# Ranks pinned to half-slots, x's first part loaded and normed first, and a second layer that sums messages with the columns on partitions

## The chip, the cores and the metric

The kernel runs on one core of a Trainium2 chip. The metric is the device time of one execution in microseconds (us). The core's engines are TensorE (PE in the profile; PEld is its weight loading), VectorE (DVE), ScalarE (ACT), GpSimd (POOL) and SyncE (SP, which only issues DMAs here). Each runs its own instructions in order; DMAs are issued from the queues of SP, ACT and POOL.

## The reference

x has 6250 nodes with 128 features. There are 106250 edges (50000 in both directions and a loop at each node), sorted by their destination, with 64 features and one of 4 types each. Everything is f32. Two layers follow each other, each behind a layer norm with ReLU and each added to x:

- The first is an attention over relations. For each of the 4 types, each of 8 heads has a logit for every edge from scores of its source and its destination; a softmax over the edges of one type into one node weighs the sources' rows, and the weighted rows are summed per node. A gelu, a product with W_cross and a second attention, over the node itself and the four types, make the node's output.
- The second makes a message of every edge and sums the messages of each node:

```
edge_in = concat([nf[src_full], nf[dst_full], ef_full])
msg = leaky_relu(edge_in @ We1) @ We2
red = segment_sum(msg, dst_full)
out = leaky_relu(concat([nf, red]) @ Wn1) @ Wn2
```

Here `src_full` is src followed by dst and `dst_full` is dst followed by src, so every edge sends a message both ways: one to its destination, by which the edges are sorted, and one to its source, by which they are not. The hidden layer of a message has 256 columns.

## The kernel before, in words

Nodes are cut into NU = 50 blocks (called units) of 126 nodes, each of two halves of 63 nodes on partitions 0 to 62 and 64 to 126. A half has up to 9 tiles (TB) of 128 edges, so there are 900 tiles. The first layer goes in NS = 25 steps of four halves. A scheduler orders the instructions of the engines from the program, within its pools of buffers; `keep_in_program_order` fixes an instruction's place among the others.

**Preparation.** SP loads src, dst, type and next destination (L161 to L239). x is loaded in 5 parts of 10 units, the first two on ACT's queue behind the weights, the rest on SP (L244 to L252). SP then writes tables to memory: e2 (L280, L281), turnd (where a node's edges end, six DMAs, L288 and L290), lacks (which edges are not of a type, four, L294) and dtyp (L297). From st0 (L345), the first edge of each half, SP reads registers (L165) and issues 100 loads of index tiles, ct (L356). The loop over the 50 units (L376 to L404) norms ten units at a time (`layernorm_relu`, L140 to L156, called at L382), transposes a unit (L384), copies it (L386), multiplies it with the weights of the four types and of the node itself (L391, L394), and writes the rows to xt on POOL's queue (L403) and the own row to memory on ACT's (L400). `columns` (L364 to L373) casts and transposes one ct tile in each of the last ten units and so makes xi, the indices that the first layer gathers with. DMAs of SP's and ACT's queues take turns on eight semaphores, so one may wait for the one before it on the same semaphore.

**First layer.** POOL issues one indirect gather of 128 rows of xt per tile (`gather0`, L85), 17 tiles ahead of their use (LA0). DVE, ACT and PE weigh them (`messages`, L603 to L618) and sum them per node. A tile of a step has two half-slots, (i, 0) inside `messages` and (i, 1) behind it, in which softmax pieces of the next step are put. Beside this the kernel works out where each message to a source shall be written in the second layer: `count` (L738), then 25 calls of `rank(g)` (L802), one for two units, each with three DVE instructions on 128x832 values, own_ (L805), a running sum (L807) and a predicated copy (L808); `ranked` (L810) ends it and writes the places (L823). `rank_at` (L825) gives the ranks to tiles (0 and, in odd steps, 5) of the steps from NCS on. Their place in the program does not keep the scheduler from moving them.

**Second layer.** For each unit and each of 9 positions there is a step with two tiles: POOL gathers rows of abtab, 7 positions ahead (AHEAD, L85), PE multiplies (L1105), DVE adds (L1107), ACT multiplies (L1108), DVE takes the maximum (L1109). The hidden row s has 512 columns, 256 for each direction. The 256 for the destination are summed at once, as a matmul with the one-hot oh (128 edges x 64 nodes) as the weights and s as the moving operand (L1125), both halves into one tile `sums` of 128 nodes x 256 columns. The 256 for the source are scattered by POOL to m2d (L1113), sorted by the places from the ranks. `windows` (L986) reads them back, part by part (DONE = 11, 22, 32, 43, 50), makes a one-hot ohw of 128 x 128 (L1015) and sums them with it as the weights (L1016). `add_sums` (L979) puts or adds a unit's sums to racc, 128 nodes x 256 columns per unit. `ready` (L1040) loads and prepares the next unit. Pieces of windows and ready are put between the steps by generators.

**Tail.** Behind the last scatter, the fifth part's windows run, and `node_update` (L905) runs for four units at a time: it transposes racc (8 transposes, L912, and 2 ACT copies to rT, L913), multiplies with We2 (L916), and makes the two layers of the node update (L922, L924, L930) and the output.

The two lines that sum messages:

```
nc.tensor.matmul(sums[q * 64:(q + 1) * 64, :], oh[:, q * TB + i, :], s[:, q, 0:HID],
                 start=(i == 0), stop=(i == TB - 1))                              # L1125
nc.tensor.matmul(sums, oh, mt[:, i, 0:HID], start=(i == 0), stop=(i == n - 1))    # L1016
```

The second operand is the weights, the third the moving operand; the output has the weights' columns on partitions.

Of the kernel before, what the change touches and what calls it, by code (L numbers as in the profile page):

```python
# [89 lines left out]
def kernel(ctx: ExitStack, tc: tile.TileContext, x, src, dst, ef, et, w_rel, a_src, a_dst,  # L90
# [107 lines left out]
    with ExitStack() as prep:  # L198
# [3 lines left out]


        wall = cpool.tile([P, R * XR + R * H + C + 2 * H], F32, name="wall")
        wx = wall[:, 0:R * XR].rearrange("p (r c) -> p r c", r=R)
# [34 lines left out]


        x_sb = cpool.tile([P, NU, C], F32, name="x_sb")
        for u0 in range(0, NU, 10):
            nc.gpsimd.memset(x_sb[:, u0:u0 + 10, :], 0.0)  # L244
            for q in range(2):
                n0 = u0 * DB + q * GB
                k = 10 if u0 + 10 < NU else 9
                xq = x[u0 * DB:(u0 + k) * DB, :].rearrange("(u q r) c -> q r u c", q=2, r=GB)[q]
                for r0, r1 in ((0, 48), (48, GB)):
                    (nc.scalar if u0 < 20 else nc.sync).dma_start(x_sb[q * 64 + r0:q * 64 + r1, u0:u0 + k, :], xq[r0:r1])  # L250
        for h, n in halves(NU - 1):
            nc.sync.dma_start(x_sb[h, NU - 1, :], x[n, :])  # L252

        nc.gpsimd.tensor_copy(wx[:, :, 0:C], wr)
# [28 lines left out]
        nc.vector.tensor_copy(dstf, ints["dst"])  # L283
        dn = cpool.tile([P, 2, J], BF16, name="dn")
        tt(dn[:, 1, :], ints["dst"], nxt, op=ALU.is_equal)
        ts_(dn[:, 0, :], dn[:, 1, :], -1.0, NEAR, op0=ALU.add, op1=ALU.mult)
        for k in range(2):
            nc.sync.dma_start(turnd[k, 1:JE + 1].rearrange("(p j) -> p j", j=J), dn[:, k, :])  # L288
            for o, w in ((0, 1), (JE + 1, 7)):
                nc.sync.dma_start(turnd[k:k + 1, o:o + w], dn[0:1, k, 0:w])  # L290
        for r in range(R):
            ne = wpool.tile([P, J], BF16, name="ne")
            ts_(ne, ints["et"], float(r), None, op0=ALU.not_equal)
            nc.sync.dma_start(lacks[r].rearrange("(p j) -> p j", j=J), ne)  # L294
        dty = cpool.tile([P, J], F32, name="dty")
        stt(dty, dstf, float(R), ints["et"], op0=ALU.mult, op1=ALU.add)
        nc.sync.dma_start(dtyp[0].rearrange("(p j) -> p j", j=J), dty)  # L297


# [59 lines left out]


        first = cpool.tile([P, NBK, TB], F32, name="first")
        nc.gpsimd.iota(first, [[GB, NBK], [0, TB]], base=0, channel_multiplier=0, allow_small_or_imprecise_dtypes=True)
# [13 lines left out]
        for u in range(NU):  # L376
            if u >= NU - NBK // CG:
                columns(u - NU + NBK // CG)
            if u % 10 == 0:
                h_sb = wpool.tile([P, 10, C], F32, name="h_sb")  # L380
                sq = wpool.tile([P, 10, C], F32, name="sq", bufs=1)
                layernorm_relu(wpool, h_sb, x_sb[:, u:u + 10, :], sq)  # L382
            tp = pp.tile([P, P], F32, name="tp")
            nc.tensor.transpose(tp, h_sb[:, u % 10, :], ident)  # L384
            hT = wpool.tile([P, P], F32, name="hT")
            nc.scalar.copy(hT, tp)  # L386
            row = wpool.tile([P, R * XR], F32, name="row", bufs=3)
            ps = pp.tile([P, 2, 512], F32, name="ps")
            xw = R * XR // 2
            for k in range(2):  # L390
                nc.tensor.matmul(ps[:, k, 0:xw], hT, wall[:, k * xw:(k + 1) * xw], start=True, stop=True)  # L391
            nc.vector.tensor_copy(row.rearrange("p (a c) -> p a c", a=2), ps[:, :, 0:xw])
            po = pp.tile([P, R * H + C + 2 * H], F32, name="po")
            nc.tensor.matmul(po, hT, wall[:, R * XR:], start=True, stop=True)  # L394
            for q in range(2):
                nc.scalar.copy(edbd[q * 64:(q + 1) * 64, u, q * 32:(q + 1) * 32], po[q * 64:(q + 1) * 64, 0:R * H])
            so = wpool.tile([P, SX], F32, name="so", bufs=3)
            nc.scalar.copy(so[:, 0:C + 2 * H], po[:, R * H:])
            nc.gpsimd.tensor_tensor(out=so[:, C + 2 * H:], in0=x_sb[:, u, :], in1=blb, op=ALU.add)
            nc.scalar.dma_start(own[u * P:(u + 1) * P, :], so)  # L400
            for q in range(2):
                n0 = u * DB + q * GB
                nc.gpsimd.dma_start(xt[n0 * R:(n0 + GB) * R, :].rearrange("(p r) c -> p (r c)", r=R),  # L403
                                    row[q * 64:q * 64 + GB, :])  # L404
# [36 lines left out]
    with ExitStack() as s1_:  # L441
# [360 lines left out]
        def rank(g):  # L802

            own_ = wp.tile([P, J], F32, name="own_", bufs=1)
            stt(own_, skey, float(g), sunit, op0=ALU.is_equal, op1=ALU.mult)  # L805
            place = wp.tile([P, J], F32, name="place", bufs=1)
            scan(place, own_, own_, base1[:, g:g + 1], op0=ALU.add, op1=ALU.max)  # L807
            nc.vector.copy_predicated(plc, own_.bitcast(I32), place)  # L808

# [14 lines left out]

        rank_at = [(s, i) for s in range(NCS, NS) for i in ((0, 5) if s % 2 else (0,))]  # L825

# [23 lines left out]
        for s in range(NS):  # L850
# [5 lines left out]
            if more:  # L856
                work(s + 1)
                for at, f in zip(((2, 0), (3, 1), (4, 0), (4, 1), (5, 0), (5, 1), (6, 0), (7, 0), (8, 0)), soft(s + 1)):
                    todo[at] = f
                for c in range(3):  # L860
                    todo[c, 1] = lambda c=c: logits(s + 1, c)
                gts.append(wp.tile([P, 2, R + 1], F32, name="gt", bufs=3))
            for i in range(TB):
                n = s * TB + i
                if n + LA0 < NS * TB:
                    gather0(n + LA0)
                messages(s, i, acc, turns_, todo.get((i, 0), lambda: None))
                todo.get((i, 1), lambda: None)()
                if more and i <= R:
                    tallies(s + 1, i, gts[s + 1])  # L870

                g = NC0 + s * TB + i
                if g < NU // 2:
                    count(g, True)
                if (s, i) == (NCS, 0):
                    counted()
                if (s, i) in rank_at[:NU // 2]:
                    rank(rank_at.index((s, i)))
                    if rank_at.index((s, i)) == NU // 2 - 1:
                        ranked()  # L880
                if i == 5 and s + 2 < NS:
                    loads(s + 2)
# [11 lines left out]
    c3 = fast.enter_context(tc.tile_pool(name="c3", bufs=1))  # L894
    racc = c3.tile([P, NU, HID], F32, name="racc")
    w2 = c3.tile([P, 2, C], F32, name="w2")
# [6 lines left out]
    def node_update(wp, pp, b0, nbs):  # L903
# [3 lines left out]
        nc.sync.dma_start(hT[:, 0:w], h2t[:, b0 * P:b0 * P + w])  # L907
        rT = wp.tile([P, 2, 4 * P], F32, name="rT")
        for a in range(2):
            tp = pp.tile([P, 4 * P], F32, name="tp")  # L910
            for i in range(nbs):
                nc.tensor.transpose(tp[:, i * P:(i + 1) * P], racc[:, b0 + i, a * P:(a + 1) * P], ident)  # L912
            nc.scalar.copy(rT[:, a, 0:w], tp[:, 0:w])  # L913
        ps = pp.tile([P, 4 * P], F32, name="tp")
        for a in range(2):
            nc.tensor.matmul(ps[:, 0:w], w2[:, a, :], rT[:, a, 0:w], start=(a == 0), stop=(a == 1))  # L916
        rdT = wp.tile([P, 4 * P], F32, name="rdT")
# [27 lines left out]
    with ExitStack() as s4:  # L945
# [33 lines left out]
        def add_sums(b, sums):  # L979

            if b in begun:
                tt(racc[:, b, :], racc[:, b, :], sums, op=ALU.add)
            else:
                nc.scalar.copy(racc[:, b, :], sums)
                begun.add(b)

        def windows(j):
# [17 lines left out]
            for b in range(NU):  # L1005
# [5 lines left out]
                ts_(at[:, 0:n], mt[:, 0:n, HID], float(-b * DB), None, op0=ALU.add)  # L1011
                sums = ps2.tile([P, HID], F32, name="sums2")
                for i in range(n):
                    oh = mp.tile([P, P], F32, name="ohw", bufs=4)
                    ts_(oh, col, at[:, i:i + 1], None, op0=ALU.is_equal)  # L1015
                    nc.tensor.matmul(sums, oh, mt[:, i, 0:HID], start=(i == 0), stop=(i == n - 1))  # L1016
                add_sums(b, sums)
                yield

        with ExitStack() as s5:  # L1020
# [64 lines left out]
            for u in range(NU):  # L1085
# [5 lines left out]
                if u in DONE[:-1]:  # L1091
# [5 lines left out]
                    taken = 0  # L1097
                sums = pt.tile([P, HID], F32, name="sums")
                for i in range(TB):
# [24 lines left out]
                    for q in range(2):  # L1124
                        nc.tensor.matmul(sums[q * 64:(q + 1) * 64, :], oh[:, q * TB + i, :], s[:, q, 0:HID],  # L1125
                                         start=(i == 0), stop=(i == TB - 1))
                    if u >= DONE[0]:
# [595 lines left out]
```

## Time and profile before

| what | us |
|---|---|
| median of 3 runs (lowest, highest) | 4111.01 (4106.76, 4119.22) |
| the profiled execution | 4104.87 |
| its span in the trace | 4103.1 |
| preparation, to the first gather | 0 to 158.7 |
| first layer, to its last gather | 158.7 to 1403.4 |
| between, to the second layer's first gather | 1403.4 to 1492.8 |
| second layer's steps, to the last scatter | 1492.8 to 3902.7 |
| tail | 3902.7 to 4103.1 |

Over the span PE is busy for 3053.0 us (74%), POOL for 2892.2 (70%), DVE for 2738.6 (67%), ACT for 1545.1 (38%). The bounds of the stages are the starts and ends of POOL's indirect DMAs in the trace. A group's line in the profile names the source line, the engine, the operation, its output and inputs and its shape, then the count, the busy time, the mean of one and the idle time of the engine just before it, with what ended that. In a timeline a line has the start, the length, and in brackets the idle time before it and what released it. Busy times of DMA instructions on POOL are the time in which POOL makes the descriptors; the names SPq and ACTq stand for the issue of a DMA.

### The profile page before, as it was taken

The numbers are of one execution on the slowest core, as the hardware profiler recorded it, in microseconds if no ns is written. First come the engines' busy times: TensorE is split into PE (matmuls) and PEld (weight loads), VectorE is DVE, ScalarE is ACT, GpSimd is POOL, SyncE is SP. The second block draws the span as 40 slices with busy tenths as digits, with TensorE's granted clock in tenths as the row PEclk, the third lists the DMA queues.
The fourth block names the chain that finished last, engine by engine and source line by source line (L and its number), as shares of the span: only waits on it lengthen the run. The fifth ranks groups of instructions, "written<-read, shape, count | busy, mean of one in ns | idle before, by whom it ended". The sixth has DMA issues, their size and how long they took to land. (4 is left out here: it accounts for less than half of the span.)

```text
span 4103.1 us, 43438 instructions
## 1 busy us (share of the span) xinstructions
PE 3053.0 (74%) x11258; PEld 1729.4 (42%) x11258; DVE 2738.6 (67%) x5139; ACT 1545.1 (38%) x2990; POOL 2892.2 (70%) x2887
## 2 busy tenths in 40 slices
PE   4468877778887756666678877778768777688888
PEld 3346555555555532222234342334324333244455
DVE  7467888887777745555466665666657666577755
ACT  3256655566666622222223333222222322222211
POOL 5777787777777527777777777777777777777600
PEclk9669978899999978888899898999989998899999
DMA  7544444455555356666587886888868878588754
GB/s 193 160 101 122 115 114 115 116 123 121 122 129 127 92 135 186 178 178 182 164 252 236 254 249 183 246 245 242 248 198 259 246 234 248 174 260 272 228 167 140
DMA packets 414557, 754.19 MB, mean 184 GB/s; under 512 B 182846, under 2 KB 249380, under 8 KB 414300
## 3 DMA queue, kind: packets, MB, share of 16 engines
q0 software_dynamic: 148800, 430.91, 35.8%
q1 hardware_dynamic: 234314, 290.32, 27.2%
q10 hardware_dynamic: 31186, 30.10, 2.6%
q8 instruction: 92, 1.51, 0.2%
q14 instruction: 165, 1.35, 0.1%
HBM read 586.37 MB, written 164.69 MB: 183 GB/s over the span
## 5 line engine op out<-in xcount | busy, mean ns | idle before, releaser
L85 POOL DMA_INDIRECT xg<-xt,xi x900 | 970.8, 1079 | 274.4 <-issue 224.6
L1113 POOL DMA_INDIRECT m2d<-s,placei x900 | 913.1, 1015 | 294.6 <-issue 211.4
L85 POOL DMA_INDIRECT ag<-abtab,srci x900 | 907.7, 1009 | 294.6 <-issue 205.4
L1105 PE MATMUL z<-rhs,lt 128*128 128x512 f32 x1800 | 1032.5, 701 | 0.6 <-ACT lt L1069 0.6
L1109 DVE TENSOR_TENSOR s<-s,z 128x1024 f32<-128x1024 f32 x450 | 548.1, 1220 | 549.1 <-ACT z L1108 547.7
L1125 PE MATMUL sums<-s,oh 128*64 128x256 f32 x1800 | 335.2, 455 | 491.3 <-DVE s L1109 490.6
L1107 DVE TENSOR_TENSOR s<-z,ag 128x1024 f32<-128x1024 f32 x450 | 549.8, 1222 | 198.8 <-PE z L1105 154.3
L617 PE MATMUL acc<-oh,msg 128*128 128x256 f32 x1800 | 534.3, 435 | 174.2 <-DVE oh L616 168.9
L1108 ACT ACTIVATE z<-s 128x1024 f32<-128x1024 f32 x450 | 461.1, 1025 | 414.8 <-DVE s L1107 413.5
L1105 PEld LDWEIGHTS z<-rhs,lt 128*128 128x128 f32 x1800 | 352.5, 216 | 447.9 <-issue 441.0
L1016 PE MATMUL sums<-mt,ohw 128*128 128x256 f32 x2024 | 523.3, 392 | 8.7 <-DVE ohw L1015 8.7
L1110 ACT COPY s<-srcf 128x2 f32<-128x2 f32 x450 | 86.7, 193 | 1175.8 <-DMA m2d<-s,placei 1159.9
L617 PEld LDWEIGHTS acc<-oh,msg 128*128 128x128 f32 x1800 | 365.2, 216 | 279.7 <-DVE oh L616 210.3
L1016 PEld LDWEIGHTS sums<-mt,ohw 128*128 128x128 f32 x2024 | 389.3, 198 | 198.0 <-issue 128.5
L1125 PEld LDWEIGHTS sums<-s,oh 128*64 128x64 f32 x1800 | 98.6, 149 | 727.6 <-DVE s L1109 579.4
L616 DVE TENSOR_SCALAR oh<-iota,key 128x256 f32<-128x256 f32 x900 | 307.6, 363 | 144.0 <-PE acc L617 136.0
L624 ACT ACTIVATE junk<-dt,nthr 128x1152 bf16<-128x1152 f32 x250 | 312.9, 1252 | 0.2
L1015 DVE TENSOR_SCALAR ohw<-col,at 128x128 f32<-128x128 f32 x1012 | 250.1, 302 | 15.6 <-PE sums L1016 7.9
L1069 ACT COPY lt<-tp 64x384 f32<-64x384 f32 x300 | 141.7, 472 | 108.0 <-PE tp L1065 55.8
L1065 PE MATMUL tp<-ident,fe 128*128 128x128 f32 x450 | 83.6, 292 | 125.5 <-ACT lt L1069 95.6
L607 DVE TENSOR_TENSOR msg<-xg,pw 128x512 f32<-128x512 f32 x225 | 150.8, 684 | 14.6 <-ACT pw L602 14.4
L542 ACT COPY es<-xg 128x128 f32<-128x128 f32 x225 | 62.1, 297 | 221.1 <-DMA xg<-xt,xi 175.8
(417 smaller groups left out, 3227.3 us busy)
## 6 DMA issues: line engine op xcount, KB each, us to landing
mt<-m2d SPq DMA_DIRECT2D x156, 514.0 KB
db<-in_dst_dram SPq DMA_DIRECT2D x200, 288.0 KB
mt<-m2d SPq DMA_DIRECT2D x53, 642.5 KB
dt<-dtyp SPq DMA_DIRECT2D x100, 288.0 KB
fe<-in_edge_attr_dram SPq DMA_DIRECT2D x100, 288.0 KB
mt<-m2d SPq DMA_DIRECT2D x41, 385.5 KB
xg<-xt,xi POOLq DMA_INDIRECT x900
ag<-abtab,srci POOLq DMA_INDIRECT x900
```

The lines of the kernel that those rows point to most:

```text
L85: nc.gpsimd.indirect_dma_start(out=o, out_offset=None, in_=table, in_offset=bass.IndirectOffsetOnAxis(ap=idx.bitcast(I32), axis=0))
L616: ts_(oh.rearrange("p t n -> p (t n)"), iota, key[:, k:k + 1], None, op0=ALU.is_equal)
L617: nc.tensor.matmul(acc[q // 2][:, :, q % 2, :], msg[:, q, :], oh, start=(i == 0 and q % 2 == 0), stop=(i == TB - 1), skip_group_check=True)
L624: nc.scalar.activation(junk, lanes[s]["dt"][v], AF.Sign, bias=nthr[:, u, t:t + 1], accum_out=g[:, v, t:t + 1])
L1015: ts_(oh, col, at[:, i:i + 1], None, op0=ALU.is_equal)
L1016: nc.tensor.matmul(sums, oh, mt[:, i, 0:HID], start=(i == 0), stop=(i == n - 1))
L1105: nc.tensor.matmul(z[:, q, :], lt[q][:, i * P:(i + 1) * P], rhs[(2 * u + q) % 4], start=True, stop=True)
L1107: tt(s[:, :, 0:2 * HID], z, ags.pop(n), op=ALU.add)
L1108: nc.scalar.mul(z, s[:, :, 0:2 * HID], 0.01)
L1109: tt(s[:, :, 0:2 * HID], s[:, :, 0:2 * HID], z, op=ALU.max)
L1113: st = nc.gpsimd.indirect_dma_start(out=m2d, out_offset=bass.IndirectOffsetOnAxis(ap=placei[:, k:k + 1], axis=0), in_=s[:, q, HID:HID + MW ...
L1125: nc.tensor.matmul(sums[q * 64:(q + 1) * 64, :], oh[:, q * TB + i, :], s[:, q, 0:HID], start=(i == 0), stop=(i == TB - 1))
```

## The change

1. x's first ten units are loaded on ACT's queue right behind the first two weight loads; the other four parts' loads follow, the second part's on ACT's queue too. h_sb holds 20 units, the first norm covers 4 units, the second 6, and the others, of ten, are called seven units ahead of their use. The buffers of hT go from 2 to 3, those of row and so from 3 to 6.
2. turnd, lacks and dtyp are made and written behind the ct loads, their writes kept in that place.
3. `rank(g)` returns three functions. Each is called in a half-slot of its own, pinned there: (0, 0), (1, 0), (2, 1), and in odd steps for a second rank (7, 1), (8, 0), (8, 1).
4. In both sums the message is now the weights, in two pieces of 128 columns, and the one-hot is the moving operand: L1125 becomes four matmuls with 64 moving columns per step, L1016 two with 128 per tile. The sums have the message's columns on partitions, so racc is 128 columns x 2 x 128 nodes per unit, and `node_update` takes it as it is: L912 and L913 go.

```diff
+        h_sb = cpool.tile([P, 20, C], F32, name="h_sb")
+        load_x(0, nc.scalar)
...
+        load_x(10, nc.scalar)
+        for u0 in range(20, NU, 10):
+            load_x(u0, nc.sync)
...
+        norm(0, 4)
...
-        dn = cpool.tile([P, 2, J], BF16, name="dn")
...
+            c = nc.sync.dma_start(turnd[k, 1:JE + 1].rearrange("(p j) -> p j", j=J), dn[:, k, :])
+            tc.keep_in_program_order(c)
...
-            if u % 10 == 0:
-                h_sb = wpool.tile([P, 10, C], F32, name="h_sb")
...
+            if u == 0:
+                norm(4, 6)
+            if u % 10 == 3 and u + 7 < NU:
+                norm(u + 7, 10)
...
-            row = wpool.tile([P, R * XR], F32, name="row", bufs=3)
+            row = wpool.tile([P, R * XR], F32, name="row", bufs=6)
...
-            nc.vector.copy_predicated(plc, own_.bitcast(I32), place)
+            return [lambda: stt(own_, skey, float(g), sunit, op0=ALU.is_equal, op1=ALU.mult),
+                    lambda: scan(place, own_, own_, base1[:, g:g + 1], op0=ALU.add, op1=ALU.max),
+                    lambda: nc.vector.copy_predicated(plc, own_.bitcast(I32), place)]
...
-        rank_at = [(s, i) for s in range(NCS, NS) for i in ((0, 5) if s % 2 else (0,))]
+        rank_at = [(s, at) for s in range(NCS, NS) for at in (((0, 0), (1, 0), (2, 1)), ((7, 1), (8, 0), (8, 1)))[:1 + s % 2]]
...
+                    if (i, h) in at:
+                        tc.keep_in_program_order(ranks[g][at.index((i, h))]())
...
-        rT = wp.tile([P, 2, 4 * P], F32, name="rT")
-        for a in range(2):
-            tp = pp.tile([P, 4 * P], F32, name="tp")
-            for i in range(nbs):
-                nc.tensor.transpose(tp[:, i * P:(i + 1) * P], racc[:, b0 + i, a * P:(a + 1) * P], ident)
-            nc.scalar.copy(rT[:, a, 0:w], tp[:, 0:w])
...
-                    nc.tensor.matmul(sums, oh, mt[:, i, 0:HID], start=(i == 0), stop=(i == n - 1))
+                    for a in range(2):
+                        nc.tensor.matmul(sums[:, a, :], mt[:, i, a * P:(a + 1) * P], oh, start=(i == 0 and a == 0),
+                                         stop=(i == n - 1), skip_group_check=True)
...
-                        nc.tensor.matmul(sums[q * 64:(q + 1) * 64, :], oh[:, q * TB + i, :], s[:, q, 0:HID],
-                                         start=(i == 0), stop=(i == TB - 1))
+                        for a in range(2):
+                            nc.tensor.matmul(sums[:, a, q * 64:(q + 1) * 64], s[:, q, a * P:(a + 1) * P],
+                                             oh[:, q * TB + i, :], start=(i == 0 and q == 0 and a == 0),
+                                             stop=(i == TB - 1), skip_group_check=True)
```

## The prediction

> **What bounds the kernel now.** I read the busy time by stage first, cutting the span where POOL's work changes: preparation, first layer's gathers, the gap before the second layer, its steps, the tail. The columns are stage, length, then busy us (instructions) of PE, PE's loads, DVE, ACT and POOL, the granted clock, DMA share and GB/s.
>
> ```profile
> 0.00:158.70 158.70, 89.57 (x377) 63.94 (x377) 110.49 (x205) 50.76 (x212) 100.05 (x184) 0.90 0.73 193
> 158.70:1403.40 1244.70, 943.17 (x4064) 656.88 (x4064) 969.94 (x2053) 753.04 (x1407) 970.75 (x900) 0.85 0.51 119
> 1403.40:1492.80 89.40, 64.27 (x278) 48.88 (x277) 55.41 (x166) 37.45 (x70) 0.60 (x5) 0.86 0.10 31
> 1492.80:3902.70 2409.90, 1776.84 (x5766) 838.57 (x5766) 1488.88 (x2333) 675.55 (x1250) 1820.83 (x1801) 0.88 0.76 225
> 3902.70:4103.10 200.40, 179.12 (x774) 121.13 (x774) 113.89 (x385) 28.32 (x52) 0.00 (x0) 0.96 0.52 155
> ```
>
> Then the costliest groups on the page (count | busy us, mean ns | idle before):
>
> ```profile
> L85 POOL DMA_INDIRECT xg<-xt,xi x900 | 970.8, 1079 | 274.4 <-issue 224.6
> L1113 POOL DMA_INDIRECT m2d<-s,placei x900 | 913.1, 1015 | 294.6 <-issue 211.4
> L85 POOL DMA_INDIRECT ag<-abtab,srci x900 | 907.7, 1009 | 294.6 <-issue 205.4
> ```
>
> In the first layer POOL's 970.8 us busy plus 274.4 idle before its gathers are the whole 1245: nearly all that idle time is issue, some 0.30 us each. So POOL sets both layers; undisturbed, a gather is 0.95 + 0.30 = 1.255 us. 900 of them need 1130 us, and 1245 were used; 1800 need 2260, and 2410 were used. In the tail POOL is idle and PE is busy for 179 of 200 us. What PE, DVE or ACT save within the layers is worth nothing unless POOL's own instructions become shorter.
>
> The timeline of the preparation (start, length) shows what holds POOL's first gather:
>
> ```profile
> 42.92 0.69 PE L384 MATMUL tp<-ident,h_sb 128*128 128x128 f32 x2 [6.92 <-DVE h_sb L156]
> ...
> 57.56 1.42 SPq L294 DMA_DIRECT2D lacks<-ne  x2
> 62.77 0.39 SPq L356 DMA_DIRECT2D ct<-e  x1
> ...
> 149.50 0.29 DVE L367 CAST ctf<-ct 90x256 f32<-90x256 int32 x1 [4.78 <-DMA abtab<-zr]
> ...
> 154.50 1.04 POOL L403 DMA_DIRECT2D xt<-row  x2
> 158.66 1.40 POOL L85 DMA_INDIRECT xg<-xt,xi  x1 [0.46 <-DMA t<-turnd]
> ```
>
> The 100 ct loads are issued from 62.77 to 146.7, 0.84 us apart; the last columns are cast at 149.50, the last block's rows go to xt at 154.50, the first gather follows at 158.66, 12 us after the last ct issue.
>
> **The change, part by part.**
>
> *Start (x first, turnd, lacks and dtyp behind ct).* st0 is cast at 38.5 and SP has written turnd's first rows by 39. One write of turnd then waits 12.1 us for a block's own rows, the other writes end at 59, and ct's first load starts 3.8 us later, after its register load. In the built program the ct loads stand directly behind e2. x's first ten units are 0.45 us of weight loads earlier and six other loads come behind them, but the statistics that end in st0 have the same work on DVE, plus earlier norms (1.5 us each) beside it. I put st0 at 42 and ct at 46, not 62.8. At 84 us the last is issued at 130; the first gather follows 12 us later, about 142. Second chain: the first transpose comes at 42.92 now, and x's first load moves from 7.40 to about 1.8, so say 37; 46 blocks took 89.4 us, 1.94 each, so the last of 50 begins about 132, and this holds the gather no later than ct does. Gain: 158.7 − 142 ≈ **−17**. It can be less: ct loads also waited 8.1 us for blocks' own writes, and more blocks may now fall among them; the bounds are −5 (blocks and ct keep each other in step) and −25 (norm of four units brings the block loop to about 25 and ct's waits go). The moved writes, 11 DMAs of 0.4 to 0.8 us, now stand between ct and the first step's four loads on SP: those come some 10 us later relative to ct's end. 17 gathers run ahead of the first message, 17 × 1.255 = 21 us, which covers it; without cover it costs the first messages up to 10 us.
>
> *Ranks.* Each of 25 ranks is three DVE instructions, 1.02 (L805), 1.95 (L807), 1.10 us (L808). They fall between 447 and 860 us, where POOL does 34 gathers in 50 us against 38 later:
>
> ```profile
> 600.00:650.00 50.00, 39.95 (x34) 0.82 0.47 109
> 1150.00:1200.00 50.00, 38.73 (x38) 0.92 0.53 129
> ```
>
> The timeline shows a gather that starts during the scan lasting 2.36 us and not 0.95:
>
> ```profile
> 498.41 1.95 DVE L807 TENSOR_TENSOR_SCAN place<-own__4354,base 128x832 f32<-128x832 f32 x1
> 498.76 2.36 POOL L85 DMA_INDIRECT xg<-xt,xi  x1 [0.30 <-DVE msg L607]
> ```
>
> By the gathers that overlap these three kinds, they lengthen POOL by about 40 us in all, 1.6 per rank. The change separates the instructions and spreads the ranks to about 1170 us; it removes none. A gather that meets a scan meets it in either place, so I take **0**. Bounds: −40 (pinned places miss the gathers, or it was bunching) and +8 (a gather is now lengthened by single instructions that formerly shared one: 25 × 0.3). Behind a pinned instruction DVE has the tile's oh and msg, at most 1.95 us late: the 17 gathers ahead cover that. The end of the ranking moves from 877 to about 1200 us, before placei is first used behind 1493; 290 us cover it.
>
> *Second layer's sums in the steps.* L1125 was 2 matmuls a step with 256 moving columns, becoming 4 with 64, with 128-column weights. An f32 matmul is two records here. The nearest row is L930, 128×128 weights with 128 moving columns:
>
> ```profile
> 3967.44 0.97 PEld L930 LDWEIGHTS ph<-wn2t,hid 128*128 128x128 f32 x8 [0.66 <-DVE hid L926]
> 3967.44 1.16 PE L930 MATMUL ph<-wn2t,hid 128*128 128x128 f32 x8 [0.42 <-DVE hid L926]
> ```
>
> Eight loads and eight matmuls in 1.16 us with the latency of the last: 0.12 per pair, loads beside matmuls. Eight records at 0.11 are 0.88 us against 0.58 now: +0.3 a step. L1016's tile was 2 records of 256 columns, 0.43 us, and becomes 4 of 128, 4 × 0.11: the same. PE's step is 1.71 (z) + 0.58 + 2.4 tiles × 0.43 + 0.2 (edge-feature transposes) ≈ 3.5 of POOL's 5.25 us; 3.9 after, hidden behind POOL. Only in the last seven steps, at about 4.2 us and bound by PE, does it show: 7 × 0.35 ≈ **+3** (0 to +30, the upper end if every PE microsecond in the last tenth of the steps counts).
>
> The Trainium skill, "TensorE: Matmul & The Clock Gate", Part 3, "The mechanism", speaks against such narrow matmuls: it says that a weight load overlaps matmuls in flight only when they use different row groups, which full 128-row matmuls don't (it also names a background weight buffer, which would allow it). L930's 0.12 us per pair is against that here; by the rule the sum would come near +50 (an estimate: loads and matmuls in turn), by the row it is −22.
>
> *Tail.* The 100 transposes L912 and 26 ACT copies L913 go. In a run of four, L912 takes 0.60 us, with two 0.38: 0.11 each, 100 × 0.11 = 11 us of PE, which was busy for 179 of 200. L916 keeps its columns. L1016's 12 tiles per four blocks cost +0.2, at 0.44 against 0.43: 12.5 × 0.2 = +2.5. Sum **−8**, from +5 (fewer gaps to fill for the in-order PE, waits for hid stay) to −15 (rT's wait goes too). ACT's copies (13.5 us) are hidden beside PE.
>
> **Sum:** −17 + 0 + 3 − 8 = −22. The profiled run took 4104.87 us (span 4103.1, 1.8 around it), 0.15% under the runs' median of 4111.01. 4104.9 − 22 = 4083; against the median 4089. I say **4086**, the middle.
>
> **The rivals.**
>
> *Start gain swallowed.* For: ct loads, own rows and x writes share queues, and one turnd write waited 12.1 us for own rows. Against: after st0 nothing else keeps ct back. Then −5 + 3 − 8 = −10: about 4098.
>
> *Ranks' stretch vanishes.* For: 34 against 38 gathers; if a lone instruction in its slot falls while POOL is between descriptors, 40 us go. Against: number and length of instructions stay, and messages lengthen gathers as well. −22 − 40: about 4045.
>
> *Weight loads not hidden (slower).* Place: the tail and the steps' PE. If load and matmul of a pair come in turn, each 0.107 us (a quarter of a tile's 0.43, and near L930's 0.97 for eight loads), a pair is 0.21 and a tile of L1016 0.86, not 0.43: 160 tiles in the tail × 0.43 = +69, and a step's PE is 1.71 + 8 × 0.16 + 2.4 × 0.86 + 0.2 = 5.25, level with POOL: +10 or so. Minus 17 and 11: about +50, 4155. It decides from 0.14 us per pair: 650 pairs in the tail × 0.03 = 20 eats the gain. For: different weights for every matmul, with only 64 columns to hide behind. Against: L930.
>
> *The change doesn't do what it says.* The built order has ct ahead of turnd, ranks apart and no L912, so only the time is open.
>
> **How the numbers follow.** Forecast (sum between −14 and −30) 0.55; start swallowed 0.2 (half of it within the bound below); ranks gone 0.1; loads not hidden 0.1; other mixtures, about nothing gained, 0.05. About 0.3%, 12 us, is what a measurement of this kernel can tell from no change. Faster: 0.55 + 0.1 + 0.1 = 0.75; within: 0.1 + 0.04 = 0.14; slower 0.11. The range takes in ranks gone (4045) at the low end and no gain at all (4112) at the high; outside it lie the third case and a few extremes.
>
> **What would show it.** Right: ct's first load near 46, the first gather near 142, first layer still about 1245 us long, but with the slow stretch thin and spread from 447 to 1170; second layer's steps still about 2410; tail about 192, its L1016 tiles at 0.43 to 0.46 us. Wrong: a first gather past 152 (start swallowed); a first layer under 1215 (ranks); L1016 tiles above 0.56 us or PE at POOL's 5.25 us in the steps (loads); a later first message than 20 us behind the first gather (SP's moved writes).

## The result, and the profile after

The changed kernel takes 4130.72 us (median of 7 runs, 4128.24 to 4138.9), the kernel before 4109.22 (7 runs): a ratio of 1.0054, 95% interval 1.0045 to 1.0064. It is 22 us **slower**; about 20 us faster was forecast, and 4130.7 lies outside the range of 4045 to 4112.

The profiled execution has a span of 4137.2 us. Cut at the same events as before, the stages are (columns as in the table of before):

```profile
0.00:151.70 151.70, 85.30 (x377) 65.83 (x377) 112.14 (x204) 50.76 (x214) 97.08 (x183) 0.92 0.77 202
151.70:1413.00 1261.30, 960.30 (x4056) 668.68 (x4057) 965.25 (x2056) 751.39 (x1404) 986.86 (x901) 0.84 0.50 117
1413.00:1505.10 92.10, 68.05 (x286) 50.94 (x285) 56.91 (x169) 39.52 (x73) 0.61 (x4) 0.85 0.10 30
1505.10:3938.60 2433.50, 1917.56 (x9272) 1311.94 (x9272) 1491.74 (x2333) 677.53 (x1250) 1824.18 (x1801) 0.87 0.76 223
3938.60:4137.20 198.60, 172.31 (x992) 128.81 (x992) 115.36 (x385) 14.82 (x26) 0.00 (x0) 0.96 0.52 156
```

The preparation is 7 us shorter, the first layer 16 longer, the gap 3 longer, the steps 24 longer, the tail 2 shorter: +34 in this execution, the longest of the seven. No part gave what was forecast, and two gave losses.

**Start.** The timeline after shows the steps of the start's sum one by one:

```profile
47.30 0.90 SPq L354 DMA_DIRECT2D ct<-e  x2
...
139.05 0.29 DVE L385 CAST ctf<-ct 90x256 f32<-90x256 int32 x1 [2.08 <-DMA ct<-e]
...
143.76 1.39 POOL L421 DMA_DIRECT2D xt<-row  x2 [5.00 <-DVE row L410]
...
147.03 0.45 SPq L375 DMA_DIRECT2D dtyp<-dty  x1
...
149.80 0.35 POOL L466 IOTA iota<- 128x256 f32 x1 [4.65 <-DMA dtyp<-dty]
151.68 1.05 POOL L85 DMA_INDIRECT xg<-xt,xi  x1 [0.72 <-issue]
```

ct's first load is at 47.3 (forecast: 46). Its last is issued at 136, so one takes 0.89 us and not 0.84. Then POOL stands idle for 4.65 us ahead of its `iota` (the instruction that writes ascending numbers), until dtyp, the last of the moved writes, has landed: POOL's first instruction of the layer waits for it, and the gathers stand behind iota. The forecast saw these writes only ahead of the first messages, where 17 gathers cover them; it did not see POOL wait.

**Groups.** Of the page's groups after, these answer to the ones shown of before:

```profile
L85 POOL DMA_INDIRECT xg<-xt,xi x900 | 986.5, 1096 | 274.6 <-issue 222.2
L85 POOL DMA_INDIRECT ag<-abtab,srci x900 | 912.0, 1013 | 307.1 <-issue 203.9
L1140 POOL DMA_INDIRECT m2d<-s,placei x900 | 912.1, 1013 | 302.3 <-issue 218.1
```

A gather of the first layer has become longer (1096 ns for 1079). In the second layer the DMA instructions have not; the idle time before them has grown, by 12.5 and 7.7 us. So the first layer's loss lies inside POOL's instructions, the second's in waits.

### The profile page after: what moved, and what is told of

The parts are those of the page before. It is cut to its first block, busy times and chain, and to the rows that moved or that the text cites. A ratio compares the mean times of both kernels' runs of the same rounds, so it can differ in the third digit from the quotient of the medians.

```text
span 4137.2 us, 50981 instructions
## 1 busy us (share of the span) xinstructions
PE 3203.5 (77%) x14982; PEld 2226.2 (54%) x14982; DVE 2741.4 (66%) x5145; ACT 1534.0 (37%) x2966; POOL 2908.7 (70%) x2887
## 4 chain that ended last, share of the span: by engine, by line
PE 27%; DMA 24%; POOL 14%; DVE 13%; issue 12%; ACT 6%; SPq 1%; ACTq 0%; DVEq 0%; POOLq 0%
DMA m2d<-s,placei 13%; PE acc L635 6%; POOL ag L85 6%; PE z L1132 5%; POOL m2d L1140 5%; DMA ag<-abtab,srci 4%; PE sums L1153 3%; DVE s L1136 3%; DMA xg<-xt,xi 3%; POOL xg L85 3%; PE sums L1042 3%; DMA mt<-m2d 3%; DVE s L1134 2%; ACT z L1135 2%; PE lg L556 2%
## 5 line engine op out<-in xcount | busy, mean ns | idle before, releaser
L85 POOL DMA_INDIRECT xg<-xt,xi x900 | 986.5, 1096 | 274.6 <-issue 222.2
L1153 PE MATMUL sums<-oh,s 128*128 128x64 f32 x3600 | 547.1, 302 | 398.2 <-DVE s L1136 397.0
L1153 PEld LDWEIGHTS sums<-oh,s 128*128 128x128 f32 x3600 | 514.2, 218 | 547.6 <-DVE s L1136 463.9
L1042 PEld LDWEIGHTS sums<-ohw,mt 128*128 128x128 f32 x4048 | 525.7, 198 | 165.3 <-issue 134.2
L1042 PE MATMUL sums<-ohw,mt 128*128 128x128 f32 x4048 | 536.8, 282 | 15.4 <-DVE ohw L1040 15.3
L1092 PEld LDWEIGHTS tp<-ident,fe 128*128 128x128 f32 x450 | 56.4, 148 | 161.2 <-ACT lt L1096 99.0
```

Source lines behind the costliest of these rows:

```text
L85: nc.gpsimd.indirect_dma_start(out=o, out_offset=None, in_=table, in_offset=bass.IndirectOffsetOnAxis(ap=idx.bitcast(I32), axis=0))
L1042: nc.tensor.matmul(sums[:, a, :], mt[:, i, a * P:(a + 1) * P], oh, start=(i == 0 and a == 0), stop=(i == n - 1), skip_group_check=True)
L1153: nc.tensor.matmul(sums[:, a, q * 64:(q + 1) * 64], s[:, q, a * P:(a + 1) * P], oh[:, q * TB + i, :], start=(i == 0 and q == 0 and a == 0) ...
```

## The experiments

Lines are numbered as in each kernel; L807 and L825 are the same scan, L1125 and L1153 the same sums. Ratios and medians stand against runs of the kernel before on the same chip (e1 to e4, e5 to e8, and e17 with e18 had three different chips); stages are of one execution each. One execution differs from the next by several us (before: 4098 to 4119 in 29 runs), so the totals rest on medians, and the stages show where.

| kernel | ratio, 95% interval | median less before's | first gather at | first layer | steps | tail |
|---|---|---|---|---|---|---|
| before | | | 158.7 | 1244.7 | 2409.9 | 200.5 |
| after | 1.0054, 1.0045 to 1.0064 | +21.5 | 151.7 | 1260.7 | 2433.4 | 198.7 |
| e1 start | 0.9998, 0.9988 to 1.0009 | −1.2 | 146.4 | 1246.9 | 2409.2 | 198.4 |
| e2 ranks | 1.0004, 0.9995 to 1.0013 | +2.6 | 156.3 | 1257.4 | 2410.4 | 200.0 |
| e3 sums | 1.0017, 1.0008 to 1.0027 | +7.1 | 156.3 | 1246.9 | 2419.7 | 200.9 |
| e4 hybrid | 0.9961, 0.9948 to 0.9974 | −14.4 | 155.9 | 1248.1 | 2406.6 | 200.0 |
| e5 after again | 1.0039, 1.0025 to 1.0053 | +15.8 | 149.7 | 1254.6 | 2431.6 | 198.0 |
| e6 start, sums | 1.0006, 0.9993 to 1.0019 | +1.3 | 150.5 | 1253.5 | 2429.6 | 197.8 |
| e7 start, ranks | 1.0019, 1.0007 to 1.0032 | +5.1 | 149.2 | 1258.4 | 2414.0 | 200.7 |
| e8 ranks, sums | 1.0037, 1.0023 to 1.0051 | +13.2 | 152.2 | 1257.5 | 2421.1 | 197.4 |
| e17 whole ranks | 0.9992, 0.9979 to 1.0006 | −4.0 | 157.2 | 1239.5 | 2411.6 | 199.2 |
| e18 sums twice | 1.0010, 0.9999 to 1.0020 | +4.2 | 155.1 | 1244.0 | 2420.9 | 198.6 |

The theory at first: ranks cost in the first layer, the changed sums in the steps, the start gives less than its 7 us. The rival: one part is innocent and its loss comes with another.

**One part alone (e1, e2, e3).** Each is the kernel before with one part's hunks of the diff above.

> Before with the start alone (x's first part first, norms of 4 and 6, more buffers, turnd, lacks and dtyp behind ct). Theory: the traces put the first gather 7 us earlier, and all behind it is before's own, so 6 to 8 us less in time, first gather near 152, first layer 1245 us long, steps 2410. Rival (the start moves the later stages too, by the order that the scheduler finds with it): the first layer's length changes by over 5 us, and the time is not below that of before.

> Before with the pinned ranks alone. Theory: the first layer's 16 us more come from the ranks' places, so the first layer takes about 1260 us and the time is 13 to 18 us longer, by gathers lengthened beside the message instructions around a rank, while those beside the rank instructions themselves keep their 40 us in all. Rival (the ranks are innocent, and the first layer's stretch comes with the start or from one execution to the next): the time within 4 us of before, the first layer at 1245.

> Before with the second layer's transposed sums alone. Theory: the steps grow by about 20 us, in waits of POOL for s and z's chain at unit ends and in the last ten steps, and the tail loses 2 us: 15 to 20 us longer in all. Rival (the forecast: hidden in the steps, 8 us less in the tail): 3 to 6 us shorter, and the steps' 24 us come from what the first layer leaves behind.

e1: the first gather is 12 us earlier in this trace (of its shortest execution of 11) and the layers are as long as before, yet the median shows −1 us, with an interval of some ±4. That meets neither the 6 to 8 us of the theory nor, in the trace, the rival's changed layer. e2: the first layer is 12.7 us longer, as expected, but the time only 2.6; the trace is of one of its longer executions. e3: steps 10 us longer, no gain in the tail, +7: half of what was expected, on the theory's side.

**Two parts (e6, e7, e8), and the whole again (e5).**

> The changed kernel once more, unaltered, for a second trace and more times on the chip of the other three. If the 14 us by which its second layer's steps are longer than with the sums alone (2433 against 2420, the same instructions in the same order there) belong to that one execution, this trace has steps of 2415 to 2425; if they belong to the kernel, about 2433 again. Time 4125 to 4133.

> The change without the pinned ranks: start and sums. If the parts add up (start -1, ranks +3, sums +7 by their medians), 6 us over before, 4116. If the missing 12 us of the whole lie between start and sums, 15 to 20 over, 4128. If ranks are in every pair that is too long, 4116 here and more in the two others.

> The change without the transposed sums: start and ranks. If the parts add up, 2 us over before, 4112. If the missing 12 us lie between start and ranks, in the first layer, 13 over, 4123, and a first layer of 1265 us.

> The change without the start: ranks and sums. If the parts add up, 10 us over before, 4120. If the missing 12 us lie between ranks and sums, about 4132; the steps would then be about 2433, although their instructions are in the same order as with the sums alone.

Each part can now be priced four times, by pairs that differ in it alone (each kernel against before on its own chip). Ranks: 2.6, 6.4 (e7 less e1), 6.1 (e8 less e3), 14.5 (e5 less e6); mean **+7**. Sums: 7.1, 2.6, 10.6, 10.7; mean **+8**. Start: −1.2, 2.5, −5.8, 2.6; mean **−0.5**. Together +15, with e5 at 15.8 (the same kernel measured 21.5 first): within their scatter the parts add up, and no special tie between two is needed, though prices from 2.6 to 14.5 for one part don't exclude one. The first layer is 1255 to 1261 us with pinned ranks (five traces) and 1244 to 1254 without (six, e17 aside). The steps are longer with the changed sums in every trace, 2420 to 2433 against 2407 to 2414. With start and sums together they are 2430 to 2433, without the start 2420 and 2421, though the second layer's instructions stand in the same order on PE, DVE and ACT in the whole change as in e3. e5 repeats the 2432, so it was not one odd execution; but e6's time is not longer than e3's. Where the start's 6 us go is **open**.

**Whole ranks (e17).** The diff against e2:

```diff
-        rank_at = [(s, at) for s in range(NCS, NS) for at in (((0, 0), (1, 0), (2, 1)), ((7, 1), (8, 0), (8, 1)))[:1 + s % 2]]
+        rank_at = [(s, at) for s in range(NCS, NS) for at in (((1, 0), (1, 0), (1, 0)), ((8, 0), (8, 0), (8, 0)))[:1 + s % 2]]
```

> Whole ranks, pinned in one half-slot each, a third time. If before takes about 4110 here: separation as the cause puts the first layer at 1245 to 1250 and the time within 4 us of before; spread or pinning as the cause, 1255 to 1260 and 3 to 8 us over. If before takes about 4750 again: 35 us over, as twice before, 45 of it in the first layer.

First layer 1239.5 us, median −4.0 (an interval that takes in 0): with the three together, the spread and the pinning cost nothing here, so the separation is the cause. That e17 also stands in other half-slots than e2 wasn't tried apart. The windows of POOL's gathers (stretch, length, busy us and count, clock, DMA share, GB/s), before, then e2, then e17:

```profile
450.00:850.00 400.00, 319.41 (x265) 0.85 0.48 111
850.00:1350.00 500.00, 385.11 (x378) 0.91 0.54 128
```

```profile
450.00:850.00 400.00, 314.43 (x281) 0.87 0.48 119
850.00:1350.00 500.00, 392.10 (x354) 0.86 0.48 118
```

```profile
450.00:850.00 400.00, 313.45 (x285) 0.83 0.50 120
850.00:1350.00 500.00, 389.09 (x365) 0.88 0.49 122
```

Spread and apart, 635 gathers in 900 us; bunched, 643; spread but whole, 650. Counted from the trace, the gathers that are lengthened by over 1 us (beyond 1.95) are 20 before, 34 in e2, 37 after, 21 in e17, and their excess 28, 42, 45 and 25 us: e2 and after have 14 and 17 us more of it than before, which is the first layer's loss (13 and 16 us). Of the counted gathers 17, 28, 28 and 5 overlap an instruction of a rank. How one comes about, in e2's timeline:

```profile
488.29 1.94 DVE L807 TENSOR_TENSOR_SCAN place<-own__4089,base 128x832 f32<-128x832 f32 x1
489.24 1.75 POOL L85 DMA_INDIRECT xg<-xt,xi  x1 [0.30 <-issue]
```

The gather starts inside the scan and ends 0.76 us after it (490.99 against 490.23); before's, shown with the prediction, ended 0.76 us after its scan too (501.12 against 500.36). So it loses what is left of the scan at its start, less 0.2 us. All 25 rank scans have such a gather, before as in e2 and e17, and it always ends 0.76 to 0.89 us behind the scan. So the scan meets one in either place; what differs is how much of the scan is left then, and what the two other instructions add. The lengthening of all gathers that overlap a rank's scan is 30 us before, 37 in e2, 24 in e17; of those that overlap only its other two, 17, 22 and 13.

**Hybrid (e4).** The windows' sums and racc are changed as in the change, L1125 stays as it was, and each unit's sums are transposed within the steps:

```diff
-                add_sums(u, sums)
+                sb = wp.tile([P, HID], F32, name="sb", bufs=1)
+                nc.scalar.copy(sb, sums)
+                tp = bank()
+                for a in range(2):
+                    nc.tensor.transpose(tp[:, a * P:(a + 1) * P], sb[:, a * P:(a + 1) * P], ident)
+                add_sums(u, tp[:, 0:2 * P].rearrange("p (a n) -> p a n", a=2))
```

> Before with the windows' sums transposed as in the change, but the step's sums (two matmuls with 256 moving columns) as before; each unit's sums are copied to SBUF by ACT and transposed by PE at the unit's end, inside the steps, so the tail still has no transposes. Theory (the step's four narrow matmuls with 128-column loads are what slows the steps): steps within 5 us of before's 2410, tail 2 to 8 us shorter, time 2 to 8 us below before. Rival (the windows' narrow tiles slow the steps): steps 2420 to 2435, as with all of the sums' change.

Steps 2406.6, median −14.4 (five runs): on this chip this version beats the kernel before, by more than was expected. Its trace, of the longest of the five, is only 2 us shorter than before's, with a tail of 200.0, so where the 14 us lie is open. The loss in the steps comes with L1125's new form and not with the windows' narrow tiles.

**Sums twice (e18).** Before, with L1125 in a loop `for d in range(2)`.

> The step's sums made twice in before's form (the sums for the destinations come out doubled), a third time. If before takes about 4110 here: PE's time per step as the cause puts the steps at 2425 to 2435 and the time 10 to 20 us over; s as the weights as the cause, steps at 2413 or below, within 3 us of before. If before takes about 4750 again: 30 to 50 us over, as twice before.

The steps are 2420.9, between the two expectations; the total +4.2, at the edge of what can be told. The steps' rows of e18, then of e3:

```profile
1489.10:3910.00 2420.90, 1943.62 (x7566) 963.71 (x7566) 1496.91 (x2333) 678.91 (x1250) 1815.65 (x1801) 0.90 0.75 224
```

```profile
1493.20:3912.90 2419.70, 1920.38 (x9272) 1316.01 (x9272) 1494.88 (x2333) 676.18 (x1250) 1819.11 (x1801) 0.87 0.75 224
```

PE is busy for 1944 and 1920 us against before's 1777, and both steps are some 10 us longer. So more PE time, in before's own form, is enough to lengthen the steps in this trace, although POOL's beat is longer than PE's work. Whether s as the weights adds to that is not settled: e18 adds 167 us of PE and costs 4, e3 adds 144 and costs 7, with intervals that overlap. Half the sums, the test for it, was not run on a chip like these.

**On two other chips (e9 to e16).** The same whole ranks and doubled sums, half the sums, and the hybrid with the output's writes on ACT's queue were first run twice on chips on which the kernel before itself takes 4787 and 4744 us. Half the sums: in e3's loop, `for a in range(2 if i in (0, TB - 1) else 1)`. Hybrid: `nc.scalar.dma_start(out[n1:n2, :], y[h, :])`.

> Before with the ranks pinned at one per step (two in odd steps), but each rank's three instructions together in one half-slot, (1, 0) or (8, 0). If it is the separation of the three that lengthens more gathers (10 us more in the first layer with them apart: 1258 against 1248 on the mean of the traces), the first layer is back at 1245 to 1250 and the time within 4 us of before. If it is the spread over 800 us, or that message instructions wait behind a pinned rank, the first layer stays at 1255 to 1260 and the time is 3 to 8 us over before.

> The sums' change alone, but in seven of a unit's nine steps only the first 128 of the 256 columns are summed for the destinations (the others' sums lack these steps), so that a step has 4 records of s as weights instead of 8: PE's part is 0.44 us there, less than the 0.58 of before. If PE's time per step is what makes the second layer's steps longer (2420 to 2433 against 2411), they are at 2411 or below and the time 0 to 5 us below before. If it is that s is the weights (a load that waits for s, matmuls behind it), the steps stay at 2420 or more.

> Before, but a step's two matmuls with the one-hot as weights are made twice (the sums for the destinations come out doubled), 0.58 us more of PE in each step, in before's own form. If PE's time per step is what costs, more than with the changed sums (0.35 us more for some 7 us): steps at 2425 to 2435, the time 10 to 20 us over before. If s as the weights is what costs, PE's 4.1 us per step stay hidden under POOL's 5.25: steps at 2413 or below, time within 3 us of before.

> The earlier version with only the windows' sums transposed and each unit's transposes inside the steps, with the output's writes moved from SP's queue to ACT's. In the changed kernel's tail mt's loads stand on SP behind output writes that wait for y, and DVE waits 24 us for mt. If that order takes the gain of the 100 transposes, the tail falls from 200 to 185 to 192 us and the time to 8 to 14 us below the same version with the writes on SP. If the tail is held by mt's transfer itself or by the chain through hid and y, it stays at 198 to 200.

> Before with each rank's three instructions pinned together in one half-slot, again, on another chip. Separation: the first layer is at 1245 to 1250 and the time within 4 us of before. Spread, or message instructions that wait behind a pinned rank: the first layer at 1255 to 1260 and 3 to 8 us over before.

> The sums' change alone with, in seven of a unit's nine steps, only the first 128 of 256 columns summed for the destinations (the other columns lack these steps), again, on another chip. PE's time per step as the cause: steps at 2411 or below, 0 to 5 us below before. s as the weights as the cause: steps at 2420 or more.

> Before with the step's two sums matmuls made twice (the sums for the destinations come out doubled), 0.58 us more of PE per step, again, on another chip. PE's time per step as the cause: steps at 2425 to 2435, 10 to 20 us over before. s as the weights as the cause: steps at 2413 or below, within 3 us of before.

> Windows' sums transposed, each unit's transposes inside the steps, and the output's writes on ACT's queue, again, on another chip. SP's order as the cause: tail at 185 to 192 us, 22 to 28 us below before (the version with the writes on SP is 14 below). mt's transfer or the chain through hid and y as the cause: tail at 198 to 200, 12 to 16 below before.

Against before on those chips: whole ranks 1.0073 and 1.0082, half the sums 1.0116 and 1.0140, twice 1.0071 and 1.0105, the hybrid 1.0108 and 1.0133, all clearly slower (intervals at most ±0.3%). Against before's trace above, both layers of gathers are 13 to 30% longer there (e13: 1595 and 2723 us), with start and tail as elsewhere; before itself has no trace on these chips. In e16, of the engines' waits:

```profile
POOL xg L85 <- issue: 404.6, 822, 18.1
POOL ag L85 <- issue: 254.9, 781, 2.3
```

A single wait of POOL without a releaser that the profile shows lasts up to 18 us; before's longest ahead of an xg was 0.3. What these engines wait for is not in the trace. Thus these eight can't be carried over to the other chips, and e17 and e18 were run for (1) separation and (2) PE time. On their own chips pinned ranks aren't free even when whole: the first layer is 1616 and 1595 us with them, 1546 to 1567 with before's own. And PE's time alone doesn't set the steps there: with half the sums (and the windows' narrow tiles) they are 2828 and 2804 us at 1889 and 1874 us of PE, with before's own sums (e9, e13) 2748 and 2723 us at 1895 and 1874. Two things more: the hybrid's gain of 14 us is not there on these chips, and its tail, which is alike on both kinds of chip, is 199.6 and 198.7 us with the output's writes taken off SP. SP's order is not what holds the tail.

## Why the prediction was wrong, by its steps

From −22 forecast to the +15 of the parts are 37 us: some 17 in the start, 13 in the sums (−5 forecast with the tail, +8 found), 7 in the ranks.

- **Start, −17 forecast.** The mechanism is right and ct begins at 47.3, but of 17 us at the first gather 7 came: 5 are ct's pace (0.89 for 0.84 us), 4 POOL's wait for dtyp. Of the time, four pairs show −0.5, and where those 7 go is open. The failed step that the trace shows is "17 gathers run ahead of the first message [...] which covers it": the moved writes stand in front of POOL's first gather too.
- **Ranks, 0 forecast, bounds −40 and +8.** "A gather that meets a scan meets it in either place" is true (25 scans of 25), but the 0 drawn from it fails: it left out how much of the scan a gather meets and what the two other instructions catch once they stand alone. The upper bound named this and sized it at 25 × 0.3 = 8; it measured 14 and 17 us of gathers (e2, after), some 7 of the time. The lower bound, that the slow stretch might vanish, stayed empty; whole ranks come nearest, 25 us in the longest gathers against 28.
- **Sums in the steps, +3 forecast.** The sizes were right: PE's time per step rose by (1917.56 − 1776.84) / 450 = 0.31 us, for 0.35 forecast. What failed is "3.9 after, hidden behind POOL": the working took PE's durations at full clock. Before's own trace has a clock of 0.81 between 1600 and 2000 us. At 1892 us, first before, then after (stretch, length, PE busy, clock, DMA share, GB/s):

```profile
1892.00:1896.00 4.00, 4.00 (x9) 0.61 0.64 198
1896.00:1900.00 4.00, 1.85 (x9) 1.00 0.55 140
```

```profile
1892.00:1896.00 4.00, 1.84 (x9) 0.50 0.61 206
1896.00:1900.00 4.00, 4.00 (x6) 0.50 0.19 66
1900.00:1904.00 4.00, 1.88 (x10) 0.93 0.47 131
```

and in the timeline after, of the same stretch:

```profile
1894.16 1.97 PE L1153 MATMUL sums<-oh,s 128*128 128x64 f32 x8 [3.80 <-DVE s L1136]
...
1895.92 4.48 PE L1132 MATMUL z<-rhs,lt 128*128 128x512 f32 x5
...
1897.98 1.23 DVE L1134 TENSOR_TENSOR s<-z,ag 128x1024 f32<-128x1024 f32 x1 [3.14 <-PE z L1132]
1899.48 1.00 POOL L85 DMA_INDIRECT ag<-abtab,srci  x1 [2.29 <-DVE s L1134]
```

PE had waited 3.8 us for s. Then at a clock of 0.50 the eight sums take 1.97 us and not 1.1, z's records 0.85 and not 0.43 us each, and z stands behind the sums in PE's order; DVE waits for z, and the gather waits 2.29 us for the buffer that DVE frees. With 0.2 for the edge features' transposes, twice (1.71 + 0.88 + 0.2) is 5.6 us, beyond POOL's beat of 5.25; twice (1.71 + 0.58 + 0.2) is 5.0, within it (an estimate for the first units, which have no windows' tiles).

  Half clock as such is not new: z's records of over 0.7 us are 348 of 1800 before, 369 after. What is new is that POOL waits more often beside it. Counted from the traces, POOL's gaps of over 0.5 us in the steps rose from 29 (49 us in all) to 44 (74 us), as much as the steps grew. Those with such a z record in the 7 us ahead rose from 12 (22 us) to 26 (41 us), the others from 17 (27) to 18 (33). It is so in all traces: with L1125 as before (e1, e2, e4, e7, e17 and before) the first kind is 5 to 15 gaps, 13 to 24 us, with the changed sums (e3, e5, e6, e8 and after) 22 to 29 gaps, 37 to 47 us, while the second kind is 21 to 27 us without and 24 to 33 us with them. So some three quarters of the loss stand beside half clock. In e18 it is 11 of 18 us more, and that half clock causes the waits was not isolated: the clock itself was never changed. The Trainium skill, "TensorE: Matmul & The Clock Gate", Part 1, "What's actually happening", has such a gate: half clock by default, full after about 3.4 us of activity. The 0.50 and 1.00 in windows of 4 us agree with the two states; nothing here measures the threshold.
- **Tail, −8 forecast, +5 to −15.** It measured −2. PE did lose 6.8 us of work (179.1 to 172.3), but its idle time rose by 5. Tail groups of PE after, with the idle time before them:

```profile
L1042 PE MATMUL sums<-ohw,mt 128*128 128x128 f32 x636 | 81.9, 280 | 14.0 <-DVE ohw L1040 13.9
L955 PE MATMUL ph<-wn2t,hid 128*128 128x128 f32 x200 | 30.9, 290 | 5.3 <-DVE hid L951 3.3 <-DVE y L963 2.1
```

Before, the wait for ohw was 8.7 us. That the transposes had filled part of it, the upper bound's "fewer gaps to fill", fits this but was not tested apart; in e4, whose tail has no transposes either, it is 200.0 us. What would have to be earlier is open; it isn't the output's writes (e12, e16).
- **The rivals.** Weight loads are hidden: the eight narrow pairs take 1.00 to 1.10 us at full clock (8 × 0.16 = 1.28 by the rival), and L1042's total in the tail is 81.9 us against 80.6. So the slower side came, but not by the rival that stood for it; its 0.1 was for a mechanism that isn't there. "Start gain swallowed" was right in size for its part (−5; −7 at the first gather), but dtyp's wait was not in it.

## What to carry to other kernels

PE, which POOL bounds here, ran one z record in five at over 0.7 us instead of 0.43, before as after: check that what is to be "hidden" also fits at the low clock, in the engine's own order. Where POOL's gathers are the bound, try long DVE instructions together rather than apart (e17 against e2; on the two slower chips whole ranks cost 34 and 35 us). A transfer that is moved back can also be waited for by whatever reuses its buffer; look for that on the bounding engine first.

## What the runs showed of the hardware

A gather that starts within a rank's DVE scan ends 0.76 to 0.89 us behind it, where an undisturbed one takes 0.95 us in all; those that start in the scan's first 0.03 us are not lengthened (four before, five in e17). The Trainium skill, "SBUF — State Buffer", "The 'DVE blocks DMA' trap (SWDGE)", names such a wait for DVE instructions in a two-port mode. Its section "A bandwidth-pool intuition that's wrong (but worth ruling out)" puts the end of a blocked DMA at about 0.115 us behind a `tensor_copy`; here it is an f32 scan, and 0.76. And the kernel before takes 4744 and 4787 us on two of the chips, 16% more than the 4107 to 4110 on the others; in the traces there, the layers with indirect DMAs are much longer, the gap between them by some 10 us, preparation and tail not at all.
